# Slice attention with two heads to a transpose, one shared set of small PSUM places, and per-step turns at both ends of a batch pipeline

## The chip, the cores and the metric

The kernel runs on one core of one Trainium2 chip. The metric is the device time of one execution in microseconds; before the change the median of three runs is 2727.98 us (2726.14 to 2728.41). The profile is of one further execution, with a span of 2730.5 us. All data are fp32.

## The reference

Thirty-two graphs of 512 nodes with 256 features pass a graph network and then a slice-attention layer, each with a layer norm ahead of it and a residual around it. Cut to what matters:

```python
def gat(inp, adj_mask, W, a):
    h = inp @ W
    f1, f2 = h @ a[:F_, 0], h @ a[F_:, 0]
    e = leaky_relu(f1[:, :, None] + f2[:, None, :], 0.2)
    if adj_mask is not None:
        e = where(adj_mask > 0, e, -9e15)
    return elu(softmax(e, axis=2) @ h)

# graph network, on layernorm(x)
o = relu(xn @ mlp1_w + mlp1_b)                       # 512 features
o = elu(gat(o, None, W_fc, a_fc)) + o
o = relu(o @ mlp2_w + mlp2_b)                        # 256 features
o = elu(gat(o, adj, W_hand, a_hand)) + o
x = x + relu(o)

# slice attention, on layernorm(x): H = 8 heads, C = 64 features, G = 64 slices
fx, xm = xn @ W_fx + b_fx, xn @ W_x + b_x            # per head: N x C
w = softmax((xm @ W_slice + b_slice) / temp)         # per head: N x G
token = (w.T @ fx) / (w.sum(nodes) + 1e-5)           # per head: G x C
q, k, v = token @ W_q, token @ W_k, token @ W_v
attn = softmax(q @ k.T / 8)                          # per head: G x G
out = w @ (attn @ v)                                 # back to the nodes
x = x + concat(out) @ W_out + b_out
```

## The kernel before

**Work.** One batch (one graph) is one round of `front` (load, norm1, mlp1, h, factors, p, pv, o1), `middle` (mlp2, h2, e, p2, pv2) and `back` (norm2, w, sums, s1T, tokens, att, vo, gg, out). Those words are the names of *steps*, set in `nc.step`; `nc.age` is the batch. Weights are folded once at the start: `weff` is W_x times W_slice, `wqk` is W_q times the transpose of W_k for two heads on the diagonal, `wvo` is W_v times W_out.

**Order.** `nc` is not the hardware but a `Recorder`: every call is only recorded, with its estimated cost and what it depends on. At the end `order()` writes the order out: a first pass schedules some batches by the table `TURNS` (one due time per step, moved by `PERIOD` for each batch); from one batch of it, number 8, the start of every operation is taken as its key; for batch b the keys are moved by b periods, and for the first three and last three batches by a further shift out of `HEAD` and `TAIL`, one number for each batch. The second pass schedules everything by these keys: on each engine, of the operations that could start, the one with the lowest key. So four batches are in flight at a time (`AHEAD = 3`), and each engine executes its list strictly as written. All instructions are issued from one line, 262 in the profile, so groups are told apart by tile names.

**Transposes.** In the middle batches the wide transposes (tiles in `FLIPPED`) don't run on TensorE: VectorE turns 32x32 blocks into a stage tile, and two rounds of DMA through a scratch in DRAM put the blocks in place (`flip`, `gather`). Batches 0 and 31 (`EDGES`) have nobody to hide the DMA behind and use TensorE transposes into tiles `tr`.

**PSUM.** Eight places: five `mm`, two `tr` (transposes), one `sm` (small: `pf` in factors, `pn` in s1T, `psc` in tokens).

**Slice attention** (steps s1T to gg). Eight heads are four pairs p. `s1` holds the weighted sums of the nodes, `s1T` their transpose. `pm` becomes the tokens, feature by slice: 16 half-array matmuls with wfx, head 2p+s on partitions 64s to 64s+63, plus the bias as two matmuls of a 4-row operand (`nrow` holds the sums of w on a diagonal). `tok` is its copy; `tokbd` and `qbd` hold the tokens and the queries of a pair on the diagonal of a 128x128 block, with zeros beside it. `psc` is the scores; `sc` the scores less their maximum; the exponential goes to the diagonal of `attbd`; `ra` is one over the row sum of attbd. In vo, four transposes turn tokbd and four attbd (each a 128x128 block, half of it zeros); the copies `tokg` and `attT` go into four matmuls `pa`, whose result goes to the diagonal of `meanbd`. In gg it is multiplied with wvo; the division by the row sum and the addition of the output bias are done there, one VectorE instruction per pair. `diagonal` copies the first 64 partitions on VectorE and the rest on ScalarE.

**Around it.** mlp2 of a batch needs o1T, which comes back from DRAM and gets o0T added on VectorE. `e` of the adjacency attention adds `f2b` (a transposed, broadcast row in a `tr` place), `h` and the mask `mbias`.

Of the kernel before, what the change touches and what calls it, by code (L numbers as in the profile page):

```python
# [7 lines left out]
F32 = mybir.dt.float32  # L8
I32 = mybir.dt.int32
AF = mybir.ActivationFunctionType  # L10
OP = mybir.AluOpType
# [5 lines left out]
    "load": -225.4, "norm1": -221.3, "mlp1": -189.8, "h": -116.6, "factors": -114.5,  # L17
    "p": -107.9, "pv": -95.7, "o1": -92.0, "mlp2": -64.3, "h2": -55.6, "e": -48.0,
    "p2": -45.0, "pv2": -16.2, "norm2": -4.3, "w": 49.4, "sums": 56.1, "s1T": 80.7,
    "tokens": 121.1, "att": 121.3, "vo": 145.5, "gg": 149.5, "out": 160.2,  # L20
}
PERIOD, SPARE = 91.1, 0.00

HEAD, TAIL = (-0.7, 1.6, 2.6), (0.1, -6.3, 142.4)
# [6 lines left out]
P = 128  # L31
# [4 lines left out]
class Recorder:  # L36
# [190 lines left out]
    def order(self):  # L227
# [17 lines left out]
        for op in self._schedule([op for op in self.ops if op.age < SAMPLE + 5], keys.get, SPARE):  # L245
            ends[op.age] = max(ends.get(op.age, 0.0), op.end)
# [3 lines left out]
        shift = dict(enumerate(HEAD)) | {last - i: s for i, s in enumerate(reversed(TAIL))}  # L250
        for (age, step), ops in steps.items():
            for i, op in enumerate(ops):
                if age >= 0:
                    turn = starts[step][i * len(starts[step]) // len(ops)]
                    keys[op] = (age - SAMPLE) * period + turn + shift.get(age, 0.0)
# [43 lines left out]
def adj_ffn_kernel(  # L299
# [54 lines left out]
    def tr_tile(shape):  # L354
        return psum.tile(shape, F32, tag="tr", name="tr", bufs=2)

    def sm_tile(shape):
        return psum.tile(shape, F32, tag="sm", name="sm", bufs=1)
# [102 lines left out]
    bfx = new("bfx", [NP, P])  # L461
    nc.scalar.dma_start(bfx, b_fx.rearrange("(p f) -> p f", p=NP))
# [16 lines left out]
    attbd = new("attbd", [P, NP, P])  # L479
    nc.gpsimd.memset(attbd, 0.0)  # L480
# [250 lines left out]
    def middle(b, o1T):  # L731
# [21 lines left out]
        for j in range(NT):  # L753
            nc.tensor.transpose(f2b[:, ts(j)], h[:, j, D + 1 : D + 2].to_broadcast([P, P]), ident)
        nc.step = "e"
# [65 lines left out]
    def back(b, x1):  # L821
# [89 lines left out]
        nrow = new("nrow", [NP, 2, NP, G], tag="tokg")  # L911
        for s in range(2):
            nc.vector.tensor_tensor(
                nrow[:, s], ident[:NP, :NP, None].to_broadcast([NP, NP, G]),
                pn[:, None, ts(s, G)].to_broadcast([NP, NP, G]), op=OP.mult,
# [6 lines left out]
        for p in range(NP):  # L922
            for k in range(KD):
                for s in range(2):
                    nc.tensor.matmul(
                        pm[ts(s, C), p, :].rearrange("c (a i) -> c a i", i=Q),
                        wfx[:, k, ts(2 * p + s, C)],
                        s1T[:, k, :].rearrange("p (a n i) -> p n a i", n=NP, i=Q)[:, p, ts(s, 2)],
                        start=(p == 0 and k == 0), stop=False,
                    )  # L930
        for s in range(2):
# [136 lines left out]
```

## Time and profile before

| what | value |
|---|---|
| median of three runs | 2727.98 us |
| profiled span, instructions | 2730.5 us, 34562 |
| DMA moved | 375.35 MB, mean 137 GB/s |
| transposes of tokbd (128 records) | 20.6 us |
| transposes of attbd (128 records) | 19.8 us |
| bias matmuls, nrow and bfx (128 records) | 21.3 us |
| head matmuls, s1T and wfx (1024 records) | 37.9 us |
| GpSimd copies to tokbd (64) | 26.1 us |
| VectorE gg out of PSUM (128) | 55.9 us, 478 ns each |
| TensorE idle before mlp2, until o1T | 7.5 us, 13 times |

A group is a set of instructions with the same tiles; its busy time counts overlapping instructions once, so that of pipelined matmuls is less than count times mean. The page's second part cuts the span into 40 slices; a digit is the busy share in tenths. In a timeline a row merges neighbouring instructions of one kind: its start, its length, and in brackets the idle time of the engine ahead of it. On TensorE the records of neighbouring rows overlap slightly, so the cost of a row is read from its start to the next row's start.

### The profile page before, as it was taken

Reading aid. Unit: us, or ns where it says so; the run is one execution under the profiler, and the core shown is the slowest. Engines: PE = TensorE matmul, PEld = TensorE weight load, DVE = VectorE, ACT = ScalarE, POOL = GpSimd, SP = SyncE. Lnnn points to the kernel's source line nnn. Section 1 sums busy time; section 2 is a strip of 40 time slices with the busy share of each in tenths; the row PEclk is TensorE's granted clock in tenths of the full one; section 3 lists DMA queues with packets and bytes.
Section 4 is the critical chain, followed back from the end, with each engine's and each line's share of the span. In section 5 each row is a group of like instructions: output and inputs, shape, how many; then the busy total and the mean of one; then the engine's idle time right before and its main releaser. Section 6 shows DMA issues by size and latency. Waiting matters only on the chain.

```text
span 2730.5 us, 34562 instructions
## 1 busy us (share of the span) xinstructions
PE 2655.7 (97%) x11965; PEld 1970.5 (72%) x11965; DVE 2096.8 (77%) x5190; ACT 1101.5 (40%) x2038; POOL 154.7 (6%) x234
## 2 busy tenths in 40 slices
PE   7999999999999999999999999999999999999886
PEld 5776677777777777777777777777777777677665
DVE  6577777887778887777887777887777887777854
ACT  2443443433444433344443444443444443444321
POOL 1000000000000000000000000000000000000000
PEclk9999999999999999999999999999999999999988
DMA  5125445554455555456545445645445545445420
GB/s 167 47 63 158 118 140 162 152 157 134 122 161 162 158 151 141 129 147 169 166 136 155 124 140 169 168 132 161 121 141 170 164 138 159 119 135 153 116 85 8
DMA packets 465078, 375.35 MB, mean 137 GB/s; under 512 B 86532, under 2 KB 382088, under 8 KB 464904
## 3 DMA queue, kind: packets, MB, share of 16 engines
q1 hardware_dynamic: 461568, 371.01, 47.8%
q10 hardware_dynamic: 3336, 2.14, 0.3%
q8 instruction: 95, 1.56, 0.2%
q14 instruction: 79, 0.65, 0.1%
HBM read 197.96 MB, written 175.11 MB: 137 GB/s over the span
## 4 chain that ended last, share of the span: by engine, by line
PE 69%; DVE 17%; DMA 8%; ACT 2%; issue 2%; SPq 1%; POOL 1%; DVEq 0%; ACTq 0%; POOLq 0%
PE mm L262 66%; DMA o1T<-scr 3%; DVE w L262 2%; PE tr L262 2%; DVE u L262 2%; DVE e L262 2%; DMA xt<-in_x_dram 2%; SPq L262 1%; DMA scr<-u_stage 1%; PE sm L262 1%; POOL ln_rstd L262 1%; DVE rs L262 1%; DVE e_stage L262 1%; DVE mx L262 1%; DVE u_stage L262 1%
## 5 line engine op out<-in xcount | busy, mean ns | idle before, releaser
L262 PE MATMUL mm<-wfc,o0T 128*128 128x257 f32 x2048 | 479.5, 380 | 0.0
L262 PE MATMUL mm<-h,pT 128*128 128x256 f32 (+1 forms) x2048 | 459.6, 380 | 2.1 <-DVE pT L262 1.5
L262 PEld LDWEIGHTS mm<-wfc,o0T 128*128 128x128 f32 x2048 | 381.4, 189 | 81.7 <-issue 32.5
L262 PEld LDWEIGHTS mm<-h,pT 128*128 128x128 f32 x2048 | 382.8, 189 | 64.2 <-DVE pT L262 4.9
L262 PE MATMUL mm<-xn,w 128*128 128x257 f32 x1024 | 264.4, 384 | 8.4 <-DVE w L262 4.3
L262 ACT COPY h<-mm 128x257 f32<-128x257 f32 (+1 forms) x384 | 143.2, 373 | 318.8 <-PE mm L262 311.0
L262 PE MATMUL mm<-gg,wT 128*128 128x256 f32 x1024 | 249.4, 380 | 0.0
L262 PE MATMUL mm<-xnT,w 128*128 128x512 f32 x512 | 244.7, 612 | 4.4 <-DMA xnT<-scr 2.5
L262 PE MATMUL mm<-o1T,w 128*128 128x512 f32 x512 | 230.3, 601 | 7.7 <-DVE o1T L262 7.5
L262 PE MATMUL mm<-h,p2T 128*128 128x257 f32 x1024 | 236.7, 382 | 0.7 <-ACT p2T L262 0.7
L262 PE MATMUL mm<-weff,xn2T 128*128 128x512 f32 x512 | 232.2, 594 | 0.2 <-ACT xn2T L262 0.2
L262 PEld LDWEIGHTS mm<-xn,w 128*128 128x128 f32 x1024 | 190.8, 192 | 36.6 <-issue 8.1
L262 PEld LDWEIGHTS mm<-h,p2T 128*128 128x128 f32 x1024 | 194.9, 191 | 30.0 <-ACT p2T L262 1.1
L262 PEld LDWEIGHTS mm<-gg,wT 128*128 128x128 f32 x1024 | 192.4, 191 | 29.4 <-issue 1.4
L262 ACT ACTIVATE u<-mm,rd 128x256 f32<-128x256 f32 x192 | 90.4, 472 | 263.3 <-DVE rd L262 191.5
L262 PEld LDWEIGHTS mm<-o1T,w 128*128 128x128 f32 x512 | 95.7, 191 | 123.1 <-issue 91.5
L262 DVE SCALAR_TENSOR_TENSOR e<-tr,h,mbias 128x512 f32<-128x512 f32 x128 | 92.4, 743 | 101.9 <-PE tr L262 101.9
L262 ACT ACTIVATE e<-e,nmax 128x512 f32<-128x512 f32 x128 | 92.4, 722 | 187.0 <-DVE nmax L262 186.0
L262 PEld LDWEIGHTS mm<-xnT,w 128*128 128x128 f32 x512 | 94.5, 195 | 99.5 <-issue 76.7
L262 DVE STREAM_TRANSPOSE o_stage<-o2T 128x512 f32<-128x512 f32 x64 | 45.5, 711 | 157.0 <-ACT o2T L262 157.0
L262 PEld LDWEIGHTS mm<-weff,xn2T 128*128 128x128 f32 x512 | 92.8, 191 | 90.3 <-issue 86.9
L262 ACT ACTIVATE m<-m 128x512 f32<-128x512 f32 x192 | 119.8, 625 | 78.6 <-DVE m L262 78.5
(150 smaller groups left out, 3938.8 us busy)
## 6 DMA issues: line engine op xcount, KB each, us to landing
scr<-xn_stage SPq DMA_DIRECT2D x240, 128.0 KB, 2.6
scr<-u_stage SPq DMA_DIRECT2D x120, 256.0 KB, 4.8
o1T<-scr SPq DMA_DIRECT2D x30, 1024.0 KB, 6.1
scr<-e_stage SPq DMA_DIRECT2D x120, 256.0 KB, 4.8
p2T<-scr SPq DMA_DIRECT2D x30, 1024.0 KB, 5.2
scr<-w_stage SPq DMA_DIRECT2D x120, 256.0 KB, 5.4
w_raw<-scr SPq DMA_DIRECT2D x30, 1024.0 KB, 5.9
xt<-in_x_dram SPq DMA_DIRECT2D x32, 512.0 KB, 4.6
```

Of the source, the lines that this page charges most:

```text
L262: getattr(getattr(self.nc, op.engine), op.method)(*op.args, **op.kwargs)
```

## The change

It has four parts.

1. *Compact attention.* The two heads of a pair no longer stand on the two partition halves of one block, but side by side in one half, in two blocks; the other half holds the next pair. So one 128x128 transpose of two blocks of `tok` has no zeros in it, turns four heads, and leaves the two heads of a pair on the two partition halves, from where `diagonal` puts them into `tokbd`: the diagonal is made after the transpose instead of before. The attention is kept in `sc` (64 wide, no zeros), normalised there by `ra`, and transposed in the same way; `attT` is one copy. `attbd` and `tokg` are gone, and gg is one addition for two blocks. GpSimd has no part in it any more.
2. *Bias in the half-array form.* `bfx` and `nrow` are padded with zeros to 128 rows, so that the bias matmuls have the tile form of their neighbours; there are four instead of two, of half the width.
3. *PSUM.* `sm` tiles are taken from `tr`, which has three places. In the two edge batches `f2b` is copied to SBUF by ScalarE, so that its place comes free for the transposes of `e`.
4. *Turns.* `TURNS` has new values, and `HEAD` and `TAIL` have a shift for each step of each of the six batches. The first pass leaves out batch 0 and the setup.

The purpose of 1 and 2 is fewer and more uniform TensorE instructions, that of 3 and 4 a better order where the pipeline fills and drains.

```diff
--- before.py
+++ after.py
@@ -14,14 +14,23 @@
 ENGINES = ("tensor", "vector", "scalar", "gpsimd", "sync")
 
 TURNS = {
-    "load": -225.4, "norm1": -221.3, "mlp1": -189.8, "h": -116.6, "factors": -114.5,
-    "p": -107.9, "pv": -95.7, "o1": -92.0, "mlp2": -64.3, "h2": -55.6, "e": -48.0,
-    "p2": -45.0, "pv2": -16.2, "norm2": -4.3, "w": 49.4, "sums": 56.1, "s1T": 80.7,
-    "tokens": 121.1, "att": 121.3, "vo": 145.5, "gg": 149.5, "out": 160.2,
+    "load": -247.8, "norm1": -132.8, "mlp1": 38.1, "h": 94.5, "factors": 94.5, "p": 98.3,
+    "pv": 111.6, "o1": 113.4, "mlp2": 134.2, "h2": 135.6, "e": 149.2, "p2": 168.3,
+    "pv2": 191.9, "norm2": 205.0, "w": 254.6, "sums": 271.5, "s1T": 283.6, "tokens": 329.1,
+    "att": 360.2, "vo": 363.9, "gg": 367.0, "out": 372.2,
 }
-PERIOD, SPARE = 91.1, 0.00
-
-HEAD, TAIL = (-0.7, 1.6, 2.6), (0.1, -6.3, 142.4)
+PERIOD, SPARE = 92.2, 0.00
+
+HEAD = (
+    (-7, -36, 9, 0, -9, -126, -38, -34, -17, 0, -18, -6, -1, -21, -25, -29, -44, 3, 3, 4, 17, 0),
...
+TAIL = (
...
+    (57, -3, -2, -3, 1, 0, 0, 1, -10, -2, 4, 0, 22, 23, -19, -66, -25, -71, -80, -54, -28, -32),
+)
 
 
 SAMPLE, SETUP = 8, 15.0
@@ -242,17 +251,19 @@
                 part += cost
         for op in steps[-1, "setup"]:
             keys[op] = SETUP
-        for op in self._schedule([op for op in self.ops if op.age < SAMPLE + 5], keys.get, SPARE):
+        first = [op for op in self.ops if 0 < op.age < SAMPLE + 5]
+        for op in self._schedule(first, keys.get, SPARE):
             ends[op.age] = max(ends.get(op.age, 0.0), op.end)
         period = (ends[SAMPLE] - ends[SAMPLE - 4]) / 4
         starts = {step: [op.start for op in steps[SAMPLE, step]] for step in TURNS}
         last = max(age for age, _ in steps)
         shift = dict(enumerate(HEAD)) | {last - i: s for i, s in enumerate(reversed(TAIL))}
+        shift = {(age, step): s for age, row in shift.items() for step, s in zip(TURNS, row)}
         for (age, step), ops in steps.items():
             for i, op in enumerate(ops):
                 if age >= 0:
                     turn = starts[step][i * len(starts[step]) // len(ops)]
-                    keys[op] = (age - SAMPLE) * period + turn + shift.get(age, 0.0)
+                    keys[op] = (age - SAMPLE) * period + turn + shift.get((age, step), 0.0)
                 else:
                     keys[op] = -SAMPLE * period + SETUP if step else -1e5
         return self._schedule(self.ops, keys.get, SPARE)
@@ -352,10 +363,10 @@
         return psum.tile(shape, F32, tag="mm", name="mm", bufs=5)
 
     def tr_tile(shape):
-        return psum.tile(shape, F32, tag="tr", name="tr", bufs=2)
+        return psum.tile(shape, F32, tag="tr", name="tr", bufs=3)
 
     def sm_tile(shape):
-        return psum.tile(shape, F32, tag="sm", name="sm", bufs=1)
+        return tr_tile(shape)
 
     EDGES = (0, B - 1)
     Q = 32
@@ -458,8 +469,11 @@
     logits(a_hand, D)
     wfx = new("wfx", [P, KD, INNER])
     nc.scalar.dma_start(wfx, W_fx.rearrange("(k p) f -> p k f", p=P))
-    bfx = new("bfx", [NP, P])
-    nc.scalar.dma_start(bfx, b_fx.rearrange("(p f) -> p f", p=NP))
+    bfx = new("bfx", [P, P])
+    nc.gpsimd.memset(bfx, 0.0)
+    nc.scalar.dma_start(bfx[:NP], b_fx.rearrange("(p f) -> p f", p=NP))
+    nrow = new("nrow", [P, 2, 2, NP // 2, G])
+    nc.gpsimd.memset(nrow, 0.0)
 
     bout = new("bout", [P, D])
     nc.sync.dma_start(bout, bcast_dram(b_out, D))
@@ -476,8 +490,6 @@
     nc.gpsimd.memset(qbd, 0.0)
     meanbd = new("meanbd", [P, NP, P])
     nc.gpsimd.memset(meanbd, 0.0)
-    attbd = new("attbd", [P, NP, P])
-    nc.gpsimd.memset(attbd, 0.0)
 
 
     mbias = new("mbias", [P, NT, N])
@@ -752,6 +764,9 @@
         f2b = tr_tile([P, N])
         for j in range(NT):
             nc.tensor.transpose(f2b[:, ts(j)], h[:, j, D + 1 : D + 2].to_broadcast([P, P]), ident)
+        if not by_dma("e", b):
+            pt, f2b = f2b, new("f2b", [P, N], tag="acb")
+            nc.scalar.copy(f2b, pt)
         nc.step = "e"
         pT = new("p2T", [P, NT, N])
         if by_dma("e", b):
@@ -908,11 +923,10 @@
 
         pn = sm_tile([NP, P])
         nc.tensor.transpose(pn, s1[:, :, D], ident)
-        nrow = new("nrow", [NP, 2, NP, G], tag="tokg")
         for s in range(2):
             nc.vector.tensor_tensor(
-                nrow[:, s], ident[:NP, :NP, None].to_broadcast([NP, NP, G]),
-                pn[:, None, ts(s, G)].to_broadcast([NP, NP, G]), op=OP.mult,
+                nrow[:NP, s], ident[:NP, None, s:NP:2, None].to_broadcast([NP, 2, 2, G]),
+                pn.rearrange("j (a o g) -> j a o g", a=2, o=1).to_broadcast([NP, 2, 2, G]), op=OP.mult,
             )
 
         nc.step = "tokens"
@@ -922,16 +936,18 @@
         for p in range(NP):
             for k in range(KD):
                 for s in range(2):
+                    pair, a = p // 2 * 2 + s, p % 2
                     nc.tensor.matmul(
                         pm[ts(s, C), p, :].rearrange("c (a i) -> c a i", i=Q),
-                        wfx[:, k, ts(2 * p + s, C)],
-                        s1T[:, k, :].rearrange("p (a n i) -> p n a i", n=NP, i=Q)[:, p, ts(s, 2)],
+                        wfx[:, k, ts(2 * pair + a, C)],
+                        s1T[:, k, :].rearrange("p (a n i) -> p n a i", n=NP, i=Q)[:, pair, ts(a, 2)],
                         start=(p == 0 and k == 0), stop=False,
                     )
-        for s in range(2):
-            nc.tensor.matmul(
-                pm[ts(s, C)], bfx[:, ts(s, C)], nrow[:, s], start=False, stop=True
-            )
+        for a in range(2):
+            for s in range(2):
+                nc.tensor.matmul(
+                    pm[ts(s, C), a::2], bfx[:, ts(a, C)], nrow[:, s, a], start=False, stop=(a == 1)
+                )
         nc.joint = False
 
         def diagonal(dst, src):
@@ -940,8 +956,6 @@
 
         tok = new("tok", [P, NP, G])
         nc.vector.tensor_copy(tok, pm)
-        for s in range(2):
-            nc.gpsimd.tensor_copy(tokbd[ts(s, C), :, ts(s, G)], tok[ts(s, C), :, :])
         pq = mm_tile([P, NP, G])
         nc.tensor.matmul(pq, wqk, tok, start=True, stop=True)
         diagonal(lambda s: qbd[ts(s, C), :, ts(s, G)], lambda s: pq[ts(s, C), :, :])
@@ -955,28 +969,28 @@
         nc.vector.tensor_tensor(
             sc, psc, amax[:, :, None].to_broadcast([P, NP, G]), op=OP.subtract
         )
-        for s in range(2):
-            nc.scalar.activation(
-                attbd[ts(s, G), :, ts(s, G)], sc[ts(s, G), :, :], AF.Exp, scale=C ** -0.5
-            )
+        nc.scalar.activation(sc, sc, AF.Exp, scale=C ** -0.5)
         ra = small("ra", [P, NP])
-        nc.vector.tensor_reduce(ra, attbd, axis=AX.X, op=OP.add)
+        nc.vector.tensor_reduce(ra, sc, axis=AX.X, op=OP.add)
         nc.vector.reciprocal(ra, ra)
+        nc.vector.tensor_tensor(
+            sc, sc, ra[:, :, None].to_broadcast([P, NP, G]), op=OP.mult
+        )
         nc.step = "vo"
 
-        pt = tr_tile([P, NP, P])
-        for p in range(NP):
-            nc.tensor.transpose(pt[:, p, :], tokbd[:, p, :], ident)
-        tokg = new("tokg", [P, NP, P])
-        nc.scalar.copy(tokg, pt)
-        pt = tr_tile([P, NP, P])
-        for p in range(NP):
-            nc.tensor.transpose(pt[:, p, :], attbd[:, p, :], ident)
+
+        pt = tr_tile([P, NP, C])
+        for q in range(NP // 2):
+            nc.tensor.transpose(pt[:, ts(q, 2), :], tok[:, ts(q, 2), :], ident)
+        diagonal(lambda a: tokbd[ts(a, G), :, ts(a, C)], lambda a: pt[ts(a, G), :, :])
+        pt = tr_tile([P, NP, G])
+        for q in range(NP // 2):
+            nc.tensor.transpose(pt[:, ts(q, 2), :], sc[:, ts(q, 2), :], ident)
         attT = new("attT", [P, NP, G])
-        diagonal(lambda s: attT[ts(s, G), :, :], lambda s: pt[ts(s, G), :, ts(s, G)])
+        nc.scalar.copy(attT, pt)
         pa = mm_tile([P, NP, G])
         for p in range(NP):
-            nc.tensor.matmul(pa[:, p, :], tokg[:, p, :], attT[:, p, :], start=True, stop=True)
+            nc.tensor.matmul(pa[:, p, :], tokbd[:, p, :], attT[:, p, :], start=True, stop=True)
         diagonal(lambda s: meanbd[ts(s, C), :, ts(s, G)], lambda s: pa[ts(s, C), :, :])
         nc.step = "gg"
         gg = med("gg")
@@ -985,11 +999,9 @@
             for s in range(2):
                 p = 2 * p2 + s
                 nc.tensor.matmul(pg[:, s, :], meanbd[:, p, :], wvo[:, p, :], start=True, stop=True)
-            for s in range(2):
-                p = 2 * p2 + s
-                nc.vector.scalar_tensor_tensor(
-                    gg[:, p, :], pg[:, s, :], ra[:, p : p + 1], bout, op0=OP.mult, op1=OP.add
-                )
+            nc.vector.tensor_tensor(
+                gg[:, ts(p2, 2), :], pg, bout[:, None, :].to_broadcast([P, 2, D]), op=OP.add
+            )
         nc.step = "out"
         for t2 in range(NT // 2):
             po = mm_tile([P, 2, D])
```

## The prediction

> **What bounds the kernel now.** I read the page's first two parts first, to see which engine is full and where it isn't.
>
> ```profile
> PE 2655.7 (97%) x11965; PEld 1970.5 (72%) x11965; DVE 2096.8 (77%) x5190; ACT 1101.5 (40%) x2038; POOL 154.7 (6%) x234
> PE   7999999999999999999999999999999999999886
> PEclk9999999999999999999999999999999999999988
> ```
>
> TensorE works 97% of the span. Its empty places are the first slice and the last three, and the last two also have a lower granted clock. The view by stretches of 91 us puts numbers on that (span, then busy time of PE, PEld, DVE, ACT, POOL, then clock, DMA share, GB/s):
>
> ```profile
> 1274.00:1365.00 91.00, 90.92 (x423) 68.51 (x423) 69.20 (x172) 37.48 (x71) 5.02 (x7) 1.00 0.57 160
> 2548.00:2639.00 91.00, 81.76 (x398) 60.95 (x399) 61.46 (x158) 31.08 (x58) 3.02 (x8) 0.92 0.39 116
> 2639.00:2730.00 91.00, 61.85 (x273) 45.35 (x271) 44.00 (x99) 18.27 (x33) 2.06 (x4) 0.83 0.05 18
> ```
>
> So there are two regimes. In the middle PE is full, and a batch costs what its PE instructions cost: "mm<-wfc x38" starts at 1303.08 and again at 1384.96 in the timeline, a period of 81.9 us. In the last two stretches 9.2 and 29.2 us of PE time stand empty. There a batch's elementwise chain sets the end. Third, PE's timeline where a middle batch does its slice attention (start, length, what, records; a plain fp32 matmul leaves two records, a transpose one; the pitch is read from start to next start):
>
> ```profile
> 1346.71 1.15 PE L262 MATMUL mm<-s1T,wfx 128*64 128x64 f32 x32
> 1347.79 0.65 PE L262 MATMUL mm<-nrow,bfx 4*64 4x256 f32 x4
> 1348.37 4.56 PE L262 MATMUL mm<-xnT,w 128*128 128x512 f32 x10
> ...
> 1355.82 0.61 PE L262 MATMUL tr<-ident,tokbd 128*128 128x128 f32 x4
> 1356.26 1.02 PE L262 MATMUL mm<-xnT,w 128*128 128x512 f32 x2
> ...
> 1357.99 0.60 PE L262 MATMUL tr<-ident,attbd 128*128 128x128 f32 x4
> 1358.42 1.03 PE L262 MATMUL mm<-wfc,o0T 128*128 128x257 f32 x4
> ```
>
> Four transposes of tokbd hold PE from 1355.82 to 1356.26, four of attbd from 1357.99 to 1358.42: 0.11 us each. The bias group nrow,bfx holds it 0.58 us. All of it is paid in full, since no gap is near. Fourth, the same timeline at the end; brackets give idle time and what ended it:
>
> ```profile
> 2652.01 1.12 PE L262 MATMUL tr<-ident,e 128*128 128x128 f32 x4 [4.05 <-ACT e L262]
> 2661.03 9.30 PE L262 MATMUL mm<-h,p2T 128*128 128x257 f32 x32 [0.68 <-ACT p2T L262]
> 2678.94 1.94 PE L262 MATMUL tr<-ident,xn 128*128 128x128 f32 x8 [8.60 <-DVE xn L262]
> 2681.12 7.73 PE L262 MATMUL mm<-weff,xn2T 128*128 128x512 f32 x16 [0.25 <-ACT xn2T L262]
> 2690.41 0.63 PE L262 MATMUL tr<-ident,w 128*128 128x128 f32 x4 [1.55 <-DVE w L262]
> ```
>
> From 2647 on only the last batch has matmuls left. Its waits between 2647.0 and 2695.8 sum to 19.6 us (those shown, three of 1.30 between the groups of e, and 0.59). The seven waits from 2548 to 2621 sum to 10.9 us (2.50, 1.17, 1.28, 0.53, 1.32, 3.30, 0.78).
>
> **What the Trainium skill says.** "TensorE: Matmul & The Clock Gate", Part 1: after an idle window of about 3.4 us the array's clock is halved until a busy window has passed. This trace agrees: the 32 records h,p2T behind the empty stretch take 9.30 us, against 7.1 us in the middle, and the clock is 0.83. Idle time at the end is thus paid twice. The same page, Part 2, says that MATMULs start in program order and only weight loads are pulled ahead: a waiting matmul holds up whatever is behind it, of any batch. "TensorEngine Tiling (Array Packing)", Key Properties: a change of tiling mode drains the array, and different tiles run in parallel. The 32 half-array records above have a pitch of 34 ns, so they do run in parallel; a drain around the 4-row bias group isn't visible as a gap.
>
> **The change, part by part.**
>
> Transposes: eight become four, since two heads' 64-wide tokens (and attention rows) fill one 128x128. 4 x 0.11 = 0.44 us of PE per batch.
>
> Bias: four records of 4x256 become eight of 128 columns in the tile form of wfx. At the pitch of wfx, doubled for the doubled columns, 8 x 0.068 = 0.54 us at most, and less if the 34 ns hold a fixed part. If the two halves didn't overlap, it would be 8 x 0.11 = 0.88. I take 0.50, so 0.08 gained (bounds -0.30 to +0.15).
>
> Together 0.52 us x 32 batches = **-16.6 us**, on the bound engine (bounds -5 to -19).
>
> Elementwise work per batch. DVE: gg from 4 x 0.478 to 2 x 0.665 (row x<-mm,x of the same size), sum of attention from 0.686 to 0.425, attT's half gone (0.41), tokbd's half added (0.41), the new product with 1/ra 0.42 (row sc<-sm): -0.42 us. ACT: one exponential less (0.41), tokg's copy gone (0.59), tokbd's half 0.37: -0.63 us. GpSimd loses its two copies (0.81), which nobody but the transposes waited for. Costed at nothing: DVE is busy 69 of 91 us in the middle and ACT 37, with PE full beside them.
>
> Order inside the attention chain. The product and its sum now stand ahead of the attention's transposes: psc to transpose grows from about 2.0 us (2707.95 to 2709.96, where nothing covers it) by 0.43 + 0.18 + 0.42 to 3.0 and, with tokbd's DVE half in between, less one exponential, still 3.0. In the changed program's order two mlp1, two transposes and three h matmuls stand there, 0.86 x 2 + 0.22 + 0.43 x 3 = 3.2 us: just covered. Between wqk and the first psc stands one mlp1 (0.86) instead of two (1.72); uncovered that step takes 1.18 us (2705.83 to 2707.01): up to 0.3 us lost. Behind attT and meanbd the weight load waits now (14.5 and 12.4 us in all); attT's two-engine copy becomes one, so up to 0.2 us is won.
>
> The wait before mlp2. Its matmuls need o1T, which goes through DRAM: last pv matmul at 1346.7, o1T usable at 1367.2, and PE arrives 0.67 us early; over the run this wait is 7.5 us in 13 places. Everything removed above, and one h matmul that moves elsewhere (0.43), lies inside this cover: 0.44 + 0.08 + 0.43 = 0.95 us less. Against it, the changed DVE order puts the copy of tok behind the last u tiles rather than ahead of them, so the last u_stage, at 1351.56 now, can leave up to 1.2 us sooner (two DVE pieces of 0.3 and the aligned waits on ACT's two exponentials). All of this together with psc I book as 0.2 us per batch x 28 = **+5.6 us** (bounds -7 if the wait vanishes, +35 for 0.95 + 0.3 per batch).
>
> PSUM: the single sm place joins the two tr places, so three are shared. No wait in the trace names sm as a short place; nothing booked.
>
> The copy of f2b is only in the two batches that take TensorE transposes. It costs each 0.58 us on ACT ahead of e, and frees a shared place for e's transposes; inside the next sum.
>
> The end. The program's order shows what the turns by step do. Before, no matmul of another batch follows the last batch's h2. After, 30's w (8 x 0.86), sums (16 x 0.43), tokens to gg (about 6) and out (16 x 0.43), and 29's gg and out (8.6) follow it: 35 us of PE work spread over the 19.6 us of waits and the chain they belong to. Not all waits close, because these pieces bring DVE work too: 30's w alone is four tiles of some 4.2 us on DVE (six rows of 0.67 to 0.70 and a reciprocal), right where the last batch's e needs it; and 30's tokens wait for a round through DRAM that only norm2's transposes and five w matmuls cover. I take 14 of the 19.6, 5 of the 10.9 ahead of it, and 5 from fewer half-clock windows (h,p2T alone loses 2.2, weff 0.7): **-24 us** (bounds 0 and -38). The last 33 us, from s to the output, stay as they are.
>
> The start. The first 8 us wait for data as before. Between w and sums of batch 1 (waits of 4.2 us from 244 to 257) stand three more h matmuls, 1.3 us: **-2 us** (bounds +3 and -5).
>
> Sum: -16.6 + 5.6 - 24 - 2 = -37.0; 2728.0 - 37.0 = **2691 us**.
>
> **The rivals.** (1) The wait before mlp2 takes the place of the removed work, and psc waits too: +35 for +5.6, so 2720. For it: the cover shrinks by more than the work. Against: only 13 of 32 batches wait at all, and the u chain can start earlier. (2) The end closes nearly completely (-38) and the wait vanishes (-7 for +5.6): 2664. For it: 35 us of filling against 30.5 of waits. Against: the added DVE work. (3) Slower: the waits of (1), and the end gains nothing, because in-order engines make the last batch queue behind 30's w and sums: 2720 + 24 = 2744. Against it: DVE is only 44 of 91 us busy there.
>
> **How the numbers follow.** Forecast 0.64, (1) 0.12, (2) 0.17, (3) 0.07. The range reaches from just above (2) to just short of (1): 2666 to 2716. Faster: forecast, (2) and most of (1), 0.88; within 0.2% 0.05; slower (3), 0.07.
>
> **What would show it.** Right: transposes out of tok and sc at 128 records in all instead of 256; a period near 81.5 in the middle; the last two stretches with 20 us less idle PE and a clock above 0.9. Wrong: waits on o1T well over 13 us in all, or on qbd or sc in every batch (then (1)); new waits on w, s or e in the last 100 us as long as the old (then the end was mis-sized).

## The result, and the profile after

The changed kernel takes **2689.97 us** (median of four runs, 2686.85 to 2691.33) against 2727.44 us for the kernel before on the same chip (four runs, 2726.14 to 2728.41). The ratio is 0.9861, with a 95% interval of 0.9844 to 0.9878: 37.5 us less, where 37.0 was forecast. The sum was met by two terms that were off in opposite directions, so that it came this close is luck. By the run old_tail below, the middle and the start gave some 5 to 9 us instead of 13, the end 29 to 32 instead of 24.

The profiled execution of the changed kernel has a span of 2685.1 us. It was the shortest of its four runs, while the profile of before (2730.5 us) is a little above its median. So differences between the two traces run up to 8 us above those between the medians. The spread of the four follows the granted clock: 2686.85 us at 0.996, 2688.72 at 0.995, 2691.22 at 0.994 and 2691.33 at 0.993.

First the page's busy times and slices, for the kernel after:

```profile
PE 2627.2 (98%) x11965; PEld 1962.5 (73%) x11965; DVE 2080.8 (77%) x5158; ACT 1089.0 (41%) x2008; POOL 90.7 (3%) x171
PE   7999999999999999999999999999999999999997
PEclk9999999999999999999999999999999999999998
```

Only one slice at the end is still below nine tenths; before there were three. The stretches of 91 us say the same in numbers (span, busy time of PE, PEld, DVE, ACT, POOL, clock, DMA share, GB/s):

```profile
1274.00:1365.00 91.00, 90.59 (x402) 66.76 (x402) 69.82 (x169) 36.42 (x68) 2.71 (x5) 1.00 0.51 148
2503.00:2594.00 91.00, 89.80 (x412) 65.90 (x411) 70.52 (x162) 36.62 (x68) 1.37 (x3) 1.00 0.37 105
2594.00:2685.00 91.00, 71.60 (x378) 55.39 (x376) 53.94 (x136) 19.36 (x38) 1.37 (x3) 0.88 0.19 58
```

Empty PE time in the last two stretches is 1.2 + 19.4 = 20.6 us, against 9.2 + 29.2 = 38.4 before. In the middle stretch it has risen, from 0.08 to 0.41 us. That is the first sign that the middle did not take the gain as forecast. The view of PE's waits names it (what waited, what for, total us, times, longest), before:

```profile
PE mm L262 <- DVE o1T L262: 7.5, 13, 1.5
```

and after:

```profile
PE mm L273 <- DVE nrow L273: 10.5, 29, 0.6
PE mm L273 <- DVE o1T L273: 0.2, 1, 0.2
```

The wait before mlp2, on o1T, is all but gone. A wait on `nrow`, the mean rows of the bias, has come, 29 times. PE's timeline of a middle batch shows where (start, length, what, records, idle before):

```profile
1337.81 2.76 PE L273 MATMUL mm<-h,pT 128*128 128x257 f32 x12
1340.41 0.27 PE L273 MATMUL tr<-ident,s 128*4 128x128 f32 x1
1340.61 1.15 PE L273 MATMUL mm<-s1T,wfx 128*64 128x64 f32 x32
1341.64 0.43 PE L273 MATMUL mm<-nrow,bfx 128*64 128x128 f32 x2
1342.43 0.65 PE L273 MATMUL mm<-nrow,bfx 128*64 128x128 f32 x6 [0.36 <-DVE nrow L273]
1343.01 2.84 PE L273 MATMUL mm<-xnT,w 128*128 128x512 f32 x6
```

The small transpose `tr<-ident,s` (pn) used to stand halfway through the 64 records of pv, h,pT. Now it stands behind all of them, right in front of the tokens. Its copies on VectorE come too late:

```profile
1341.21 0.37 DVE L273 TENSOR_TENSOR nrow<-ident,tr 4x256 f32<-4x256 f32 x1
1341.51 0.47 DVE L273 TENSOR_SCALAR u<-mm,rd 128x256 f32<-128x256 f32 x1
1341.91 0.16 DVE L273 BATCH_NORM_AGGREGATE ln_mv<-ln_st 128x2 f32<-128x6 f32 x1
1342.00 0.38 DVE L273 TENSOR_TENSOR nrow<-ident,tr 4x256 f32<-4x256 f32 x1
```

The bracket gives 0.36 us, but from 1341.64 to 1343.01 the bias group holds PE for 1.37 us. In batch 30, without a wait, the same eight records hold it for 0.54 (2630.34 to 2630.88). The loss is thus 0.83 us per batch, more than twice what the bracket shows; in 26 batches the group takes the same 1.37 us. The Trainium skill, "Perfetto Trace Analysis", Tensor Engine Instruction, says why one cannot trust the bracket alone: a matmul's end in the profile is computed from its size, not seen. This trace agrees: the records of this group are given 273 ns each (median), and without a wait they follow each other at 0.068 us.

At the end, waits of the last batches that the prediction showed have other work in them or are gone:

```profile
2605.96 7.12 PE L273 MATMUL mm<-xn,w 128*128 128x257 f32 x32
2618.01 0.38 PE L273 MATMUL tr<-ident,s 128*4 128x128 f32 x1 [4.93 <-DVE s L273]
2619.98 1.98 PE L273 MATMUL tr<-ident,xn 128*128 128x128 f32 x8 [1.60 <-DVE xn L273]
2623.36 6.08 PE L273 MATMUL mm<-weff,xn2T 128*128 128x512 f32 x10 [1.40 <-ACT xn2T L273]
2665.51 0.66 PE L273 MATMUL tr<-ident,sc 128*128 128x128 f32 x2 [2.96 <-DVE sc L273]
```

32 records of batch 30's w, xn,w, now stand ahead of the last batch's norm2. The waits of 4.05 us on e and of 8.60 us on xn have given way to these of 4.93, 1.60 and 1.40.

### The profile page after: what moved, and what is told of

It reads as the page before. It is cut to its first block, busy times and chain, and to the rows that moved or that the text cites. A ratio compares the mean times of both kernels' runs of the same rounds, so it can differ in the third digit from the quotient of the medians.

```text
span 2685.1 us, 34224 instructions
## 1 busy us (share of the span) xinstructions
PE 2627.2 (98%) x11965; PEld 1962.5 (73%) x11965; DVE 2080.8 (77%) x5158; ACT 1089.0 (41%) x2008; POOL 90.7 (3%) x171
## 4 chain that ended last, share of the span: by engine, by line
PE 66%; DVE 21%; DMA 8%; ACT 2%; issue 2%; SPq 1%; ACTq 0%; DVEq 0%; POOL 0%
PE mm L273 63%; DVE u L273 4%; PE tr L273 3%; DMA scr<-s_stage 2%; SPq L273 1%; DVE m L273 1%; DVE x L273 1%; DVE pT L273 1%; DVE u_stage L273 1%; DVE xn_stage L273 1%; DVE ln_st L273 1%; DVE xn L273 1%; DMA x<-in_x_dram 1%; DMA xt<-in_x_dram 1%; DMA out_dram<-x 1%
## 5 line engine op out<-in xcount | busy, mean ns | idle before, releaser
L273 PE MATMUL mm<-h,pT 128*128 128x257 f32 (+1 forms) x2048 | 455.8, 379 | 0.8 <-DVE pT L273 0.8
L273 PE MATMUL mm<-xnT,w 128*128 128x512 f32 x512 | 257.5, 614 | 3.4 <-ACT xnT L273 2.7
L273 PE MATMUL mm<-xn,w 128*128 128x257 f32 x1024 | 252.9, 381 | 7.4 <-DVE rs L273 4.9
L273 PE MATMUL mm<-gg,wT 128*128 128x256 f32 x1024 | 233.1, 380 | 0.0
L273 PEld LDWEIGHTS mm<-xn,w 128*128 128x128 f32 x1024 | 183.8, 190 | 42.1 <-issue 10.9
L273 DVE SCALAR_TENSOR_TENSOR e<-tr,h,mbias 128x512 f32<-128x512 f32 x120 | 86.5, 742 | 100.5 <-PE tr L273 100.5
L273 ACT ACTIVATE m<-m,neg 128x512 f32<-128x512 f32 x192 | 137.9, 718 | 4.3
L273 DVE SCALAR_TENSOR_TENSOR u<-m,u 128x512 f32<-128x512 f32 x192 | 128.0, 667 | 5.7 <-ACT m L273 5.5
```

The lines of the kernel that those rows point to most:

```text
L273: getattr(getattr(self.nc, op.engine), op.method)(*op.args, **op.kwargs)
```

## The experiments

The kernel after is the base of all of them; "+" is the experiment. Ratios are to the kernel before on the same chip.

### Which part pays: the old turns with the new attention, and the old end alone

**compact_old_turns** keeps parts 1 to 3 of the change and puts back all of part 4: the old table of turns, one shift for each batch, and the old first pass:

```diff
-    "load": -247.8, "norm1": -132.8, "mlp1": 38.1, "h": 94.5, "factors": 94.5, "p": 98.3,
...
+    "load": -225.4, "norm1": -221.3, "mlp1": -189.8, "h": -116.6, "factors": -114.5,
...
+HEAD, TAIL = (-0.7, 1.6, 2.6), (0.1, -6.3, 142.4)
```

> The new attention, bias and PSUM places with the old table of turns, the old one shift per batch and the old first pass. Theory (the attention's gain is TensorE work, the end's gain is the turns): 0.5 us a batch less TensorE work, no wait of the bias matmuls for nrow because the transpose that feeds it stands in the middle of pv as before, and an end as long as before: 2708 to 2714, the idle time of the last 91 us near 28 us. Rival A (the shorter attention chain also shortens the end): below 2700. Rival B (what the attention saves returns as a wait before mlp2, since that wait lies behind it): 2722 to 2728, waits on o1T above 15 us.

Measured: 2737.16 us, 1.0055 (1.0042 to 1.0068), *slower* than before. PE's waits:

```profile
PE mm L262 <- DVE w L262: 30.8, 31, 4.4
PE tr L262 <- DVE xn L262: 16.7, 2, 8.5
PE mm L262 <- DVE o1T L262: 3.9, 5, 1.2
```

The middle is no shorter (81.46 us a batch, 81.50 before): a new wait on w, 0.7 to 0.9 us in nearly every batch, stands where the removed work stood. The rest of the loss is at the end: the output of batch 27 is issued at 2470.9 (before 2469.6), and the end follows 272 us later instead of 261. The time lies above all three expectations, and the wait on o1T, by which the second rival was to be known, stayed small. So fewer PE instructions in an order not made for them gain nothing.

**old_tail** keeps everything, the new middle and start too, and puts back only the three old shifts of the last batches:

```diff
-TAIL = (
-    (-5, -8, -8, -1, -17, 10, 0, 5, 0, 0, -60, 0, 0, 10, 2, 0, -1, 6, 0, 10, -10, 0),
...
+TAIL = ((0.1,) * 22, (-6.3,) * 22, (142.4,) * 22)
```

> The changed kernel with the old three numbers for the last three batches (0.1, -6.3, 142.4 for every step of each); everything else as changed. Theory (some 30 us of the gain are the end's): 2714 to 2722, the last batch alone on TensorE from its e onward as before. Rival (the end is shorter because the attention's chain is, and the turns matter little): 2690 to 2698.

Measured: 2719.03 us, 0.9980 (0.9974 to 0.9987). So attention, PSUM, bias, new middle and new start together are worth 5.6 us against the before of its own chip, and the turns of the last three batches 29 us (2719.0 - 2690.0; 32 by the two ratios). The old shifts were made for the old table, but they fare no worse here than before: from the output of batch 25 to the end it is 424.1 us, against 428.7. The PSUM places and the copy of f2b were not tried alone. The busy times and the last 182 us of this run:

```profile
PE 2638.7 (97%) x11965; PEld 1970.2 (72%) x11965; DVE 2085.8 (77%) x5158; ACT 1090.4 (40%) x2008; POOL 91.0 (3%) x171
```

```profile
2538.00:2629.00 91.00, 81.13 (x390) 61.17 (x391) 62.00 (x159) 29.61 (x56) 1.47 (x4) 0.89 0.39 117
2629.00:2720.00 91.00, 61.47 (x282) 45.66 (x281) 43.17 (x97) 18.66 (x34) 1.26 (x2) 0.82 0.06 22
```

PE executes the same 11965 records of the same instructions here as in after, in 2638.7 instead of 2627.2 us. These 11.5 us are the clock's part: the same work takes longer at half clock. The clock's own record agrees. At the end, PE's records fill 35.5 us of half-clock time in old_tail and 12.7 in after; if half of that is loss, it is 17.8 against 6.3, so 11.4. The rest of the two spans is empty PE time, 2719.3 - 2638.7 = 80.6 against 2685.1 - 2627.2 = 57.9 us: 22.7 us, of which 39.4 - 20.6 = 18.8 are in the last 182.

### The new wait: mean rows early, and the bias in its old four rows

**nrow_early** takes the order as planned and moves two things in batches 1 to 30: the pn transpose 12 TensorE instructions up, its two copies 4 VectorE instructions up.

```diff
+    def early(self, order, matmuls, vectors):
...
+                to = same[-back]
...
-        for op in self.order():
+        for op in self.early(self.order(), 12, 4):
```

> The changed kernel's written order, in which for batches 1 to 30 the transpose of the sums' last column goes 12 TensorE instructions earlier and the two VectorE products nrow 4 VectorE instructions earlier; nothing else is moved. The bias group, 1.37 us from start to start with its wait in it, should fall to 0.54. Theory 1 (that 0.83 us is partly cover for the wait before mlp2, whose slack is 0.26 us): 0.25 us a batch won, 2680 to 2685, and waits on o1T come back with 10 to 20 us. Rival 1 (all of it is won): 2663 to 2669. Rival 2 (nothing is won, the wait only moves): 2688 to 2692.

Measured: 2692.92 us, 0.9885 (0.9873 to 0.9898), no gain. The wait is gone and its price with it. But two others take its place:

```profile
PE tr L287 <- ACT qbd L287: 15.5, 26, 1.0
PE mm L287 <- DVE o1T L287: 10.6, 11, 1.4
```

```profile
1342.51 0.61 PE L287 MATMUL mm<-nrow,bfx 128*64 128x128 f32 x8
1343.05 2.84 PE L287 MATMUL mm<-xnT,w 128*128 128x512 f32 x6
1345.73 0.59 PE L287 MATMUL mm<-tok,wqk 128*128 128x256 f32 x2
1346.16 1.02 PE L287 MATMUL mm<-xnT,w 128*128 128x512 f32 x2
1347.79 0.43 PE L287 MATMUL tr<-tok,qbd 128*128 128x64 f32 x2 [0.61 <-ACT qbd L287]
```

From 1342.51 to 1343.05 the bias group costs 0.54 us; PE arrives at the queries so much earlier, and waits for their copy. What is saved at one place is paid at the next: PE is not what sets the period here.

**bias_four_rows** takes back the padding of `bfx` and `nrow` to 128 rows:

```diff
-    bfx = new("bfx", [P, P])
-    nc.gpsimd.memset(bfx, 0.0)
...
+    bfx = new("bfx", [NP, P])
...
+    nrow = new("nrow", [NP, 2, 2, NP // 2, G])
```

> The changed kernel with the bias operands cut back to 4 rows, in four matmuls of 128 columns as changed: only the tile form of the bias matmuls goes back. Theory (the form matters little, what counts is columns): within 3 us of the changed kernel, the bias group in the last batch at 0.54 us. Rival (going from the 128x64 form to another and back drains the array, some 0.1 to 0.3 us each time): 4 to 15 us slower, with the group's pitch longer at its start or end.

Measured: 2692.55 us, 0.9882 (0.9868 to 0.9897); the interval overlaps that of after. The group costs nearly the same in both forms (busy time, mean ns, idle before):

```profile
L273 PE MATMUL mm<-nrow,bfx 4*64 4x128 f32 x256 | 32.6, 286 | 9.8 <-DVE nrow L273 9.7
```

With 128 rows it was 33.0 us busy and 10.5 idle. In batch 30, without a wait, four rows take 0.58 us and 128 rows 0.54; with the wait it is mostly 1.31 against 1.37. The uniform tile form is worth nothing that shows here.

### Is it VectorE? Work added to it, and work taken from it

After these four runs my theory was a loop: VectorE's gapless work of some 55 us from one batch's e to the next batch's last u_stage, then 13.4 us through DRAM to o1T, then mlp2 and h2. Two runs double an instruction in its place in the order, with unchanged results; two move work to another engine and let the planner order it anew.

```diff
# stats_twice
+            again = 1 <= op.age <= 28 and op.step == "norm1" and op.method == "bn_stats"
+            for _ in range(2 if again else 1):
# o_stage_twice
+            again = 1 <= op.age <= 28 and op.step == "p2" and op.method == "transpose"
# pv2_on_scalar, in elu_elu of the second attention
+            nc.scalar.activation(u[:, cols0], v0, AF.Copy, scale=rd0)
# add_on_gpsimd
+                (nc.gpsimd if 3 <= b < 27 else nc.vector).tensor_tensor(u3, u3, r3, op=OP.add)
```

> The changed kernel's written order, in which norm1's four bn_stats of batches 1 to 28 are executed twice: 4 x 0.34 us more of VectorE per batch, somewhere between the batch's e and its successor's last u_stage. Theory (the middle is a loop of 55 us of VectorE without a gap from e to the last u_stage, 13.4 us of DRAM round, and 12 us of mlp2, h2 and their transposes; TensorE is full beside it): the whole 1.36 us x 28 = 38 us are paid, 2726 to 2732. Rival (TensorE bounds the middle, and VectorE, busy 77%, hides it): 2690 to 2700.

> The same with the two o_stage transposes of batches 1 to 28 executed twice: 2 x 0.63 us more of VectorE per batch, but between mlp2 and the next e, where the timeline shows VectorE idle. Theory (loop): nothing is paid, 2688 to 2694. Rival A (VectorE's whole sum counts): 2722 or more. Rival B (TensorE bounds): 2688 to 2694 as well; only the pair with the doubled bn_stats tells A, B and the loop apart.

> The changed kernel with both halves of u in pv2 scaled on ScalarE, where the first half was VectorE's: 2 x 0.39 us of VectorE less per batch inside the 55 us, 2 x 0.38 more on ScalarE. Same computation. Theory (loop): the period of the middle falls from 81.3 by 0.4 to 0.8 us until TensorE's own sum is the bound, so 2668 to 2680. Rival (TensorE bounds, or its wait for nrow does): 2686 to 2694.

> The changed kernel with the four additions u+r of pv2 on GpSimd for batches 3 to 26: 4 x 0.36 us of VectorE less per batch in the 55 us. Same computation; the planner then orders the last batches differently, so only the middle is to be read. Theory (loop): the period of the middle falls by 0.6 to 0.8 us to TensorE's sum, near 80.5. Rival 1 (TensorE or its waits bound it): it stays at 81.3. Rival 2 (a GpSimd addition of 128x256 takes several microseconds and delays x1, norm2 and w): it rises above 82.

Measured:

| run | us | ratio, 95% interval | middle, us a batch |
|---|---|---|---|
| stats_twice | 2742.57 | 1.0053 (1.0039 to 1.0067) | 83.4 |
| o_stage_twice | 2692.39 | 0.9868 (0.9855 to 0.9882) | 81.4 |
| pv2_on_scalar | 2754.63 | 1.0098 (1.0084 to 1.0111) | 81.8 |
| add_on_gpsimd | 2761.88 | 1.0125 (1.0112 to 1.0139) | 82.5 |

The first two part the cases well. Four statistics of 0.42 us a batch (1.66 us), ahead of the u tiles in VectorE's queue, cost more than their length, 52.6 us in all where the theory had 38. Most batches take 83.0 us, 1.75 more than those of after. Three of the 17 take 84.8: behind the longer wait on nrow the clock falls to half for 3.41 us (from 872.2, 1206.7 and 1541.2 in the trace). Two transposes of 0.71 us (1.42 us), in a place where VectorE waits for PE anyway, cost nothing that shows. So *where* VectorE works counts, not how much. In stats_twice the wait on nrow grows with it:

```profile
PE mm L275 <- DVE nrow L275: 38.3, 52, 1.2
```

The other two tell little of the middle. A change of engine makes the planner write another order, and the fitted shifts of the last batches no longer suit it: between the outputs of batches 28 and 29 of pv2_on_scalar lie 142 us (2526.8 to 2668.8), between those of 29 and 30 of add_on_gpsimd 112. The middle of add_on_gpsimd, 82.5, is above the 82 of its second rival, though an addition took 0.77 us on GpSimd and not several. Whoever changes an operation in this kernel must fit the turns again, or keep the order.

### The same with the order kept

So three runs keep the order of after as it stands, and edit only while it is issued:

```diff
# adds_left_out
+            if 3 <= op.age <= 26 and op.step == "pv2" and op.method == "tensor_tensor":
+                continue
# pv2_in_place; pv2_sums_in_place has ('pv2', 'sums')
+            scaled = op.engine == "vector" and op.method == "tensor_scalar" and op.step in ('pv2',)
+            if scaled and 1 <= op.age <= 28 and isinstance(op.args[2], bass.AP):
+                self.nc.scalar.activation(op.args[0], op.args[1], AF.Copy, scale=op.args[2])
+                continue
```

> The order of the kernel after is kept as written, but the four additions of u and the residual before each batch's second softmax are left out for batches 3 to 26 (the outputs then lack that residual), at 0.36 us each: VectorE has 1.44 us a batch less to do inside its gapless stretch from e to the u stage, and TensorE loses nothing. Theory (the middle is a loop of 55 us of VectorE, 13.4 us round through DRAM, and 13 us of mlp2 and transposes, with TensorE's own sum near 80.5 us just beneath it): the period falls from 81.3 to TensorE's sum, 0.6 to 0.8 us a batch for 24 batches, 2671 to 2677 us. Rival (TensorE with its small waits is the bound, VectorE's length doesn't matter): 2687 to 2693. If the stretch alone were the bound and TensorE had room: 24 times 1.44, 2655.

> Same computation and same written order as the kernel after, but both halves of the u scaling of the second attention go from VectorE to ScalarE in batches 1 to 28, in the same place in the order: about 0.8 us a batch less in VectorE's stretch, and a hop to ScalarE and back. Loop theory: the period falls by 0.4 to 0.8 us, 2668 to 2680 us. Rival 1 (TensorE bounds): 2687 to 2693. Rival 2 (ScalarE takes the scaling late, behind its queue, and VectorE waits for it): the period rises by 0.3 us or more, 2698 us or more.

> As the run with the u scaling on ScalarE, and the four scalings of the first attention's sums go to ScalarE as well, in the same place: a further 4 times 0.38 us out of VectorE's stretch. Loop theory: VectorE's stretch is then 2 us shorter, TensorE's sum near 80.5 us bounds, 2668 to 2678 us. Rival 1 (TensorE bounds already): 2687 to 2693. Rival 2 (the hops to ScalarE cost VectorE or TensorE a wait of over 0.3 us a batch): 2698 us or more.

Measured: adds_left_out 2681.02 us, 0.9826 (0.9806 to 0.9845); pv2_in_place 2686.77, 0.9846 (0.9832 to 0.9861); pv2_sums_in_place 2692.79, 0.9868 (0.9852 to 0.9884). In the last of them VectorE's busy time is 59.8 us shorter (2021.0 against 2080.8 by the pages), 2.1 us for each of the 28 batches, and the period is no shorter (81.46 against 81.34); VectorE only idles 2.3 us more inside the stretch that I had called its loop (3.03 against 0.76), and the stretch is as long as it was (55.06 against 54.94). Most of that idle time is spent waiting for ScalarE, which now does the work, so this run shortens nothing and cannot decide on the loop.

adds_left_out can, since there the work is gone, and with it the residual that is added behind the second attention, in batches 3 to 26: 0.98 us less work inside the stretch made it only 0.28 us shorter, and VectorE waits more, mostly for the u tiles (0.35 us for ScalarE's half of u, 0.12 for PE's products). So the length of VectorE's own work alone does not set the period. The period fell by 0.3 us a batch for 1.44 us of instructions taken out, and the wait on nrow shrank:

```profile
PE mm L275 <- DVE nrow L275: 4.4, 13, 0.6
```

The bracket hides what is left of it: in most batches the bias group shows no wait at all there and still takes 1.11 us instead of 0.54.

**both_short** joins nrow_early with adds_left_out.

> Two earlier edits at once: the mean-row transpose and its VectorE copies moved up in the written order (alone 2692.9 us, no gain over 2690), and the four u additions of the second attention left out for batches 3 to 26 (alone 2681.0; the outputs lack that residual). Theory (two limits within 0.5 us of each other: VectorE's loop through DRAM at 81.3 us a batch, and TensorE's own sum, 80.8 with the mean rows late and 80.6 with them early): with both shortened the period falls to 80.6 to 80.8, 2671 to 2679 us, with waits on TensorE under 0.3 us a batch. Rival 1 (the early copies stretch VectorE's loop or delay the qbd and o1T tiles whatever else is shortened, as when moved alone): no gain over the additions alone, 2681 to 2690. Rival 2 (neither limit: the DRAM round or a planned order fixes the period at about 81): 2681 as with the additions alone, the mean-row wait gone and another wait of the same length in its place.

Measured: 2692.04 us, 0.9873 (0.9853 to 0.9892), no gain: the first rival, with a time just above its bounds. Its waits are those of nrow_early:

```profile
PE tr L289 <- ACT qbd L289: 11.7, 23, 1.0
PE mm L289 <- DVE o1T L289: 8.8, 10, 1.9
```

### What the middle is

With all runs at hand I split the period at two points of PE's timeline: the start of mlp2, and the first wfx matmul, which is the end of pv. Means over 17 middle batches, in us, worked out from the start and end times of these instructions in the traces; "VectorE's lag" is from the end of pv to the start of the last scaling u<-mm,rd, "o1T ready" the end of the first addition to o1T, both counted from the end of pv.

| run | period | mlp2 to end of pv | end of pv to mlp2 | VectorE's lag | last u_stage done | o1T ready |
|---|---|---|---|---|---|---|
| before | 81.50 | 61.46 | 20.05 | 1.16 | 5.65 | 19.92 |
| after | 81.34 | 61.74 | 19.60 | 0.92 | 5.06 | 19.15 |
| nrow_early | 81.52 | 61.80 | 19.72 | 1.37 | 5.51 | 19.61 |
| adds_left_out | 81.04 | 61.74 | 19.31 | 0.67 | 4.78 | 18.82 |
| both_short | 81.38 | 61.80 | 19.58 | 1.21 | 5.36 | 19.47 |
| pv2_sums_in_place | 81.46 | 61.74 | 19.72 | 1.05 | 5.19 | 19.27 |
| stats_twice | 83.41 | 62.22 | 21.19 | 2.19 | 6.33 | 20.78 |

From mlp2 to the end of pv PE works without a gap of any size, 61.7 us. What varies is the stretch behind, and there two chains of nearly equal length run side by side, both tied to VectorE's u tiles. One is the round: VectorE's lag, 4.1 us to the last u_stage, 13.4 through DRAM, 0.7 for the addition; mlp2 cannot start before it. The other is PE's own work there, *which is where the slice attention lies, from the head matmuls to wvo*, with the wait on nrow in it, whose second copy stands behind the last scaling in VectorE's queue. In before, nrow_early and both_short mlp2 starts 0.11 to 0.13 us after o1T is ready, in 14, 16 and 17 of the 17 batches within 0.12: the round ends last. In after it starts 0.45 us later, and within 0.12 in only 4 batches: PE, held up by nrow, ends last.

PE's own work is read from the shortest batches, those in which it has no other wait. Before, they take 81.06 us without any wait. After, they take 81.26 with the 0.83 of nrow in them, so 80.43 without. Some 0.63 us of PE work a batch is thus gone, as the change meant. But the average before was 0.44 above its shortest batches, for o1T, and after it is 0.83 + 0.08 above PE's own work: -0.63 - 0.44 + 0.91 = -0.16 us is all that the period gained.

Read in this way, the rest fits. Removed attention matmuls shorten only one of the chains. Nrow early frees PE, but its two copies then stand ahead of the u tiles, where VectorE is late already, and lengthen the round: in nrow_early the last scaling comes 1.37 us after pv, and ScalarE's exponential, which the second copy used to cover, becomes a gap:

```profile
1343.42 0.43 DVE L287 TENSOR_SCALAR m<-u 128x512 f32<-128x512 f32 x1
1344.01 0.69 DVE L287 SCALAR_TENSOR_TENSOR u<-m,u 128x512 f32<-128x512 f32 x1 [0.16 <-ACT m L287]
```

And VectorE's work has a one-sided price. The lag at the end of pv is only 0.9 us, so work taken off can win no more than what is left of it, while added work lengthens it: plus 1.66 us made the lag 1.27 longer and the usual batch 1.75, minus 1.44 us made the lag 0.25 shorter and the batch 0.30.

This reading, with two chains side by side, was made from the runs, after the last of them. It is argued, not shown: no run was made to test it. The test would be to make the mean rows on an engine that has no u tiles in its queue, which shortens both chains at once. As an estimate from the table that would be worth some 0.3 us a batch (o1T ready at 19.15 plus 0.12, against 19.60), 10 us in all. It was not tried. Of the versions that were, none with the whole computation beats the kernel after by more than the intervals.

## Why the prediction was right, and where not

- *"In the middle PE is full, and a batch costs what its PE instructions cost."* This is the step that failed. PE is full 99.5% of the time, and yet a batch's cost is set by 61.7 us of PE and then by the later of two chains. PE's own work of 80.43 us is less than any middle batch took. The period before was 81.5 on average, not 81.9 as read from one batch, which has a wait of 0.67 on o1T in it.
- *Transposes, -0.44 us.* Right as a count and as a duration: tokbd and attbd with sc held PE 1.31 us a batch, tok and sc hold it 0.87 (from start to next start). tr<-ident,tok has 64 records and sc 64 more than before, 128 in all.
- *Bias, -0.08 us.* The price of the form was right (0.54 for 0.58, inside the bounds). What was missed is the wait: from 0.58 to 1.37 us, outside every bound. The cause is in the new order, not in the form. I had looked at where the attention chain's operations moved, but not at pn's transpose, and had not asked what VectorE does in front of its copies.
- *Elementwise work at nothing.* Right where VectorE waits for PE (1.42 us more cost nothing there), wrong as a rule: stats_twice shows that 1.66 us at the wrong place cost 1.75 in the usual batch and 2.1 on average, with the clock's part.
- *Attention chain.* The widths of 3.0 and 3.2 us were right: sc's transposes don't wait in the middle.
- *The wait before mlp2: cover 0.95 less, u tiles up to 1.2 us sooner, booked +5.6.* The two opposing effects were right, their balance was not: 5.6 more was booked and 7.3 less came. The u tiles are done 0.59 us sooner (5.65 to 5.06), o1T 0.77, and the wait fell from 7.5 to 0.2 us. The cover shrank as forecast: in the shortest batches from 19.66 to 19.53 us, or 18.70 without nrow's 0.83, 0.96 for 0.95. But the h matmul that "moves elsewhere" (0.43) moved in front of the end of pv and lengthened the other part, 61.46 to 61.74. With nrow's loss, the period fell by 0.16 instead of 0.34: over 22 batches, from the output of batch 3 to that of batch 25, 4.0 us by the traces, where 22 x 0.34 = 7.5 was forecast.
- *Start, -2.* The output of batch 3 is issued at 504.5 instead of 508.9: -4.4.
- *End: "14 of the 19.6", "5 of the 10.9", "5 from fewer half-clock windows".* The waits were right: 38.4 - 20.6 = 17.8 us for 19. The clock was the mis-sized term. PE's records fill 31.8 us of half-clock time at the end before and 12.7 after; half of the difference, an estimate, is 9.5 us for 5. For old_tail, which differs from after in the end alone, the same reckoning gives 11.4 and the busy times 11.5. I had priced two groups at half clock (2.2 and 0.7) and a little more, and not the whole of what runs behind every long wait. The Trainium skill, "TensorE: Matmul & The Clock Gate", Part 1, has the rule, and the waits that closed (8.60 and 4.05) are longer than its window of about 3.4 us; I applied it to too few groups, and the last section shows that shorter waits count too.
- *The rivals.* Waits in place of removed work, rival 1, came true in part, on nrow and not on o1T. In compact_old_turns waits take the place of all of it, but on w and not where rival 1 had them. Of rival 2 the wait on o1T did vanish, but the end did not close: 19.4 us are still empty in the last stretch. Of rival 3 nothing came.

## What to carry to other kernels

An engine that is 99% busy can still not be the limit: split the period at the points where its in-order list meets a round through another engine or DRAM, and compare, in each part, its own work with the round beside it. Work removed from the side that isn't last comes back as a wait at the next place, and the place is no clue to the cause; at the end of a pipeline, price all work behind a long wait at the lower clock. When an order is written out by a planner with fitted turns, test a change of one operation in the kept order, or refit the turns; otherwise the end tells of the fit and not of the operation.

## What the runs showed of the hardware

- A wait in the middle of a group of small matmuls costs PE more than its bracket: 0.83 us from start to start for a bracket of 0.36 in 26 batches of after, and 0.57 us with no bracket at all in most batches of adds_left_out.
- The clock falls without one long wait, too. In 4 us stretches around the last batch's tokens, with the columns as before:

```profile
2660.00:2664.00 4.00, 1.59 (x12) 1.09 (x10) 1.59 (x4) 0.91 (x3) 0.00 (x0) 1.00 0.00 0
2664.00:2668.00 4.00, 1.98 (x8) 1.61 (x9) 1.02 (x3) 0.61 (x2) 0.00 (x0) 0.50 0.00 0
2668.00:2672.00 4.00, 3.04 (x10) 2.41 (x10) 0.69 (x2) 0.37 (x1) 0.00 (x0) 0.50 0.01 4
2672.00:2676.00 4.00, 4.00 (x15) 3.35 (x14) 1.11 (x2) 0.00 (x0) 0.00 (x0) 0.72 0.00 0
```

  The longest wait here is the 2.96 us on sc. The clock falls 1.44 us into it, at 2663.99, and in the 3.41 us ahead of that PE has 1.33 us of work on record. Half clock lasts for 10.24 us, the last 3.41 of them with PE full again. The page on the clock gate, named above, has the clock fall after an idle window of about 3.4 us; here a window that was in part busy was enough. In the traces of all fourteen kernels the clock changes on a grid of 3.41 us. Counted on that grid, every window at full clock with less than 1.41 us of PE work was followed by half clock, none with more than 2.43 us was, and in between both happened. What decides in between was not tried.
- Switching PE between 128-row and 4-row operands has no visible price. The Trainium skill, "TensorEngine Tiling (Array Packing)", Key Properties, says that a change of tiling mode drains the array; the bias group took 32.6 us in four rows and 33.0 in 128, and the runs 2692.6 and 2690.0 us, so here a drain is too small to see: the 0.04 us between 0.58 and 0.54 in batch 30 is all that is left for it.
- The way of o1T through DRAM, from the last u_stage to the first addition, is nearly constant: 13.3 to 13.8 us on average in each of the fourteen kernels.
